# Second attention layer: context read feature-major from DRAM instead of transposed on TensorE

## Chip, cores and metric

The kernel runs on one core of one Trainium2 chip, as one launch. The metric is the device time of a run in microseconds, and the time of a version is the median of its runs. All data are float32 except the attention mask bias.

## The reference

A stream `x` of 8 batches x 512 tokens x 512 features goes through four stages, each adding its result to `x`. Two stages are cross-attention to the same context, `ctx_1024`, of 8 batches x 120 keys x 512 features:

```python
x = x + tanh(g_xattn[0]) * L0_xattn(layernorm(x), ctx, ctx)          # 16 heads of 32
x = x + tanh(g_ffn[0])   * L0_ffn(layernorm(x))                      # routed experts
x = x + tanh(g_xattn[1]) * L1_xattn(layernorm(x), ctx, ctx, mask)    # the same, with mask and biases
x = x + tanh(g_ffn[1])   * L1_ffn(layernorm(x))                      # channel mix

# both attention layers, from the same ctx, with their own weights:
k = split_heads(ctx @ Wk.T + bk);  v = split_heads(ctx @ Wv.T + bv)
attn = softmax(q @ k.T / sqrt(32), masked);  out = (attn @ v) @ Wo.T + bo
```

The context does not change between the two layers; only the weights do.

## The kernel before

The four stages run one after the other on the core; `x` (32 tiles of 128 tokens x 512 features) stays in SBUF. `CrossAttention` is built twice, once for each attention layer. Its constructor does what comes before the loop over token tiles: `load` (L260) puts all loads of the layer on the queue of the SP engine, in the order written; `project_keys` (L321) makes the transposed context `ctxT` and from it the transposed keys `kT`; then come the layer-norm of the first tiles, `make_mask`, the sums of query weights on GpSimd (`sum_query_weights`, L426), and `prologue` (L376), which projects the values of a batch at a time (`project_values`, L357) between transposes of `x` and the first queries.

The context arrives token-major: 120 keys on the partitions, 8 batches x 512 features in each (`ctx`, loaded in two halves of four batches, L278). TensorE contracts over partitions, so both projections need the features on the partitions. For each batch, four transposes by the identity (L327) fill one PSUM tile `ctps`, and a copy takes it to `ctxT`: on VectorE for even batches (L334), on ScalarE for odd ones (L332). After every fourth batch, the keys of these four batches are computed (L342): four PSUM tiles `kps`, each of four matmuls of 480 columns, evicted by ScalarE (L351 in the second layer, L355 in the first). `project_values` later uses the same `ctxT` as the stationary operand, a batch at a time (L361).

In the constructor of either layer the order of all engines is the written one (`tc.manual_schedule(engines=every)`): each engine takes its instructions in this order, and an instruction that waits holds back what is behind it. SBUF pools are stacked: `ctx`, `wk` and `mrow` lie in a pool (`at_k`) that is given up after `project_keys` and the mask, `ctxT` and `bv` in one (`at_v`) given up after the prologue. A load into a place that was in use before waits for its last user. In the second layer these users are those of the expert stage that ends just before: its matmuls `l2ps` (L959), the transposes `rps` (L992), the scatter matmuls `ops` with `permT` (L1013) and the updates of `x` after them (L1021).

Other names that matter: `wv`, `wq`, `wo`, `wk` are the layer's weights, 1 MB each; `bqk`, `bv`, `gbo` its biases; `mrow` the mask, from which VectorE makes `mbias` (L316). `stats_of_batch` runs the layer-norm sums of four tiles on VectorE (L49, L50) and their scales on GpSimd (L58 to L64). `normalize` makes `xn` on ScalarE (L406), and in the second layer GpSimd then adds the output bias to `x` (L410). `queries` multiplies by `wq` and its sums (L149).

Of the kernel before, what the change touches and what calls it, by code (L numbers as in the profile page):

```python
# [9 lines left out]
FP = mybir.dt.float32  # L10
I32 = mybir.dt.int32
BF = mybir.dt.bfloat16
AF = mybir.ActivationFunctionType
# [4 lines left out]
P = 128  # L18
B, S, D = 8, 512, 512
LK = 120  # L20
# [3 lines left out]
NC = D // P  # L24
# [3 lines left out]
SM_SCALE = 1.0 / math.sqrt(HD)  # L28
# [178 lines left out]
class CrossAttention:  # L207
# [5 lines left out]


    def __init__(
        self, cm, tc, es, ins, gate, mask=None, biases=None, loads=(), then=None, vpool=None
    ):
        self.cm, self.nc, self.tc, self.gate, self.then = cm, cm.nc, tc, gate, then
        self.masked, self.biased = mask is not None, biases is not None
        nc = cm.nc  # L220

        def pool(name, bufs, **kw):
            pool = tc.tile_pool(name=name, bufs=bufs, reuse_waits="tile", **kw)
            return es.enter_context(pool)

        self.pool = pool("at_w", 1)
        vpool = vpool or self.pool
        self.norm = pool("at_n", 2)
        self.soft = pool("at_soft", 2)
        self.p_mm = pool("at_mm", 4, space=PSUM)  # L230
        self.p_s = pool("at_s", 2, space=PSUM)
        self.wq = self.pool.tile([P, NC, D], FP, name="wq")
        self.wo = self.pool.tile([P, NC, D], FP, name="wo")
        self.kT = self.pool.tile([P, NC, B * LK], FP, name="kT")
        self.v = [vpool.tile([P, 2, D], FP, name=f"v{q}") for q in range(B // 2)]
        self.xn, self.xnT, self.qT, self.probs, self.aT = {}, {}, {}, {}, {}
        self.ops = {}

        def right(name):
            return tc.tile_pool(name=name, bufs=1, side="right", reuse_waits="tile")  # L240

        with right("at_v") as self.vp:
            with right("at_k") as self.kp:
                self.load(ins, list(loads), mask, biases)
                if self.biased:
                    self.scale_biases()
                self.project_keys()
                if self.biased:
                    nc.gpsimd.tensor_scalar(self.gbo, self.gbo, self.gate, None, ALU.mult)
                for t in range(2):  # L250
                    self.normalize(t)
                if self.masked:
                    self.make_mask()
                self.sum_query_weights()
                for b in (1, 2):
                    self.stats_of_batch(b)
            self.work = pool("at_work", 2)
            self.prologue()

    def load(self, ins, loads, mask, biases):  # L260

        nc, kp, vp = self.nc, self.kp, self.vp
        ctx_in, wqT, wkT, wvT, woT = ins
        self.ctxT = vp.tile([P, NC, B * LK], FP, name="ctxT")

        wv = self.soft.tile([P, NC * D], FP, name="wv", tag="pr")
        self.wv = wv.rearrange("p (c f) -> p c f", c=NC)
        if self.biased:
            self.bv = vp.tile([LK, D], FP, name="bv")
        self.ctx = kp.tile([LK, B, D], FP, name="ctx")  # L270
        self.wk = kp.tile([P, NC, D], FP, name="wk")
        if self.masked:
            self.mrow = kp.tile([P, B, LK], I32, name="mrow")
        ctx_in = ctx_in.rearrange("b k d -> k b d")

        def half(h):
            bs = slice(h * B // 2, (h + 1) * B // 2)
            nc.sync.dma_start(out=self.ctx[:, bs, :], in_=ctx_in[:, bs, :])  # L278

        def weights(w, w_in):  # L280
            nc.sync.dma_start(out=w, in_=w_in.rearrange("(c p) f -> p c f", p=P))

        half(0)
        weights(self.wk, wkT)
        half(1)
        if self.biased:
            bqk_in, bv_in, bo_in = biases
            self.bqk = self.pool.tile([P, 2, NC], FP, name="bqk")
            nc.sync.dma_start(out=self.bqk, in_=bqk_in)
        weights(self.wv, wvT)  # L290
        if loads:
            loads.pop(0)()
        if self.biased:
            nc.sync.dma_start(out=self.bv, in_=bv_in.partition_broadcast(LK))
        if self.masked:
            nc.sync.dma_start(out=self.mrow, in_=mask.partition_broadcast(P))
        if self.biased:
            self.gbo = self.pool.tile([P, D], FP, name="gbo")
            nc.sync.dma_start(out=self.gbo, in_=bo_in.partition_broadcast(P))
        weights(self.wq, wqT)  # L300
        if loads:
            loads.pop(0)()
        weights(self.wo, woT)
        for more in loads:
            more()
# [13 lines left out]


    def project_keys(self):  # L321
        nc, ident = self.nc, self.cm.ident
        half = B * LK // 2
        for b in range(B):
            ps = self.p_mm.tile([P, NC, LK], FP, name="ctps", tag="mm")
            for c in range(NC):
                nc.tensor.transpose(  # L327
                    ps[:, c, :], self.ctx[:, b, c * P : (c + 1) * P], ident[:LK, :LK]
                )
            dst = self.ctxT[:, :, b * LK : (b + 1) * LK]  # L330
            if b % 2:
                nc.scalar.copy(dst, ps)  # L332
            else:
                nc.vector.tensor_copy(dst, ps)  # L334
            if b == B - 1:
                self.stats_of_batch(0)
            if b % 4 == 3:
                h = b // 4
                for f in range(NC):
                    ps = self.p_mm.tile([P, half], FP, name="kps", tag="mm")  # L340
                    for c in range(NC):
                        nc.tensor.matmul(  # L342
                            ps,
                            self.wk[:, c, f * P : (f + 1) * P],
                            self.ctxT[:, c, h * half : (h + 1) * half],
                            start=(c == 0),
                            stop=(c == NC - 1),
                        )
                    dst = self.kT[:, f, h * half : (h + 1) * half]
                    if self.biased:  # L350
                        nc.scalar.activation(  # L351
                            dst, ps, AF.Identity, bias=self.bqk[:, 1, f : f + 1], scale=SM_SCALE
                        )
                    else:
                        nc.scalar.activation(dst, ps, AF.Copy, scale=SM_SCALE)  # L355

    def project_values(self, b):  # L357
        nc = self.nc
# [992 lines left out]
def flamingo_kernel(ctx: ExitStack, tc: tile.TileContext, a: dict, out: bass.AP):  # L1351
    nc = tc.nc
    const = ctx.enter_context(tc.tile_pool(name="const", bufs=1))
    ident = const.tile([P, P], FP, name="ident")
    make_identity(nc, ident)
    gates = const.tile([P, 4], FP, name="gates")
# [9 lines left out]
        )  # L1366

    cm = Common(nc, const, x, ident)

    engines = mybir.EngineType  # L1370
    compute = {engines.PE, engines.DVE, engines.Activation, engines.Pool}
    every = compute | {engines.SP}
    with ExitStack() as es:
        ffn = RoutedFfn(
            cm, tc, es, gates[:, 2:3],
            [a[n] for n in ("wc", "bc", "tie", "w1", "b1", "w2", "b2")],
        )
        loads = [lambda b=b: load_x(b) for b in range(B)]
        with ExitStack() as at:
            with tc.manual_schedule(engines=every):  # L1380
                attention = CrossAttention(
                    cm, tc, at, [a[n] for n in ("ctx", "wq0", "wk0", "wv0", "wo0")],
                    gates[:, 0:1], loads=loads, then=ffn.in_slot,
                    vpool=ffn.vpool,
                )
            with tc.manual_schedule(engines={engines.PE}):
                attention.run()
            with tc.manual_schedule(engines=compute):
                attention.tail()
        ffn.run()  # L1390
    with ExitStack() as es:
        mix = ChannelMix(
            cm, tc, es, [a[n] for n in ("wr", "wk", "wv", "mu")], gates[:, 3:4], out
        )
        with tc.manual_schedule(engines=every):
            attention = CrossAttention(
                cm, tc, es, [a[n] for n in ("ctx", "wq1", "wk1", "wv1", "wo1")],
                gates[:, 1:2], a["mask"], (a["bqk"], a["bv"], a["bo"]), then=mix.in_slot,
            )
        with tc.manual_schedule(engines={engines.PE, engines.SP}):  # L1400
            attention.run()
        with tc.manual_schedule(engines=compute):
            attention.tail()
            mix.run()
# [63 lines left out]
```

## Time and profile before

| | us |
|---|---|
| median of 3 runs | 1436.9 (1434.19 to 1437.84) |
| the profiled execution, own time | 1433.48 |
| its span, first to last instruction | 1431.7 |
| start of the second layer's key stage (its first transposes) | 690.65 |
| end of that stage (first value matmul) | 721.58 |

The span is cut into what each engine did. Busy times, of the span: TensorE matmuls 97%, VectorE 72%, ScalarE 54%, GpSimd 45%. The mean granted TensorE clock is 0.998. The 16 DMA engines moved 69.46 MB, most of it at the start and between the stages. The second layer's loads land in two bursts: `ctx` and `wk` from 664.68 on, when the last `l2ps` matmul lets them, and `wv` to `wo` between 688.60 and about 705.

A line of a timeline or of a chain begins with the start and the length of a piece in us; "x16" counts instructions. A float32 matmul leaves two records, so the 16 key matmuls of a half appear as 32. A "chain of waits" is followed back from the last instruction, at each step to what released it.

### The profile page before, as it was taken

The numbers are of one execution on the slowest core, as the hardware profiler recorded it, in microseconds if no ns is written. First come the engines' busy times: TensorE is split into PE (matmuls) and PEld (weight loads), VectorE is DVE, ScalarE is ACT, GpSimd is POOL, SyncE is SP. The second block draws the span as 40 slices with busy tenths as digits, with TensorE's granted clock in tenths as the row PEclk, the third lists the DMA queues.
The fourth block names the chain that finished last, engine by engine and source line by source line (L and its number), as shares of the span: only waits on it lengthen the run. The fifth ranks groups of instructions, "written<-read, shape, count | busy, mean of one in ns | idle before, by whom it ended". The sixth has DMA issues, their size and how long they took to land.

```text
span 1431.7 us, 32559 instructions
## 1 busy us (share of the span) xinstructions
PE 1384.2 (97%) x13728; PEld 1068.2 (75%) x13728; DVE 1025.1 (72%) x1457; ACT 772.3 (54%) x1874; POOL 643.9 (45%) x576
## 2 busy tenths in 40 slices
PE   7999999999999998999999999999998999999997
PEld 3577777777776787888557777777776788888886
DVE  2666777777777676777576777777778588887786
ACT  1256666666666445444225665666656555445543
POOL 1425545545443001555375665665646333343331
PEclk9999999999999999999999999999999999999999
DMA  9200000000001347433301000000000000000001
GB/s 300 107 9 24 24 23 23 24 23 16 24 31 46 127 135 231 120 105 87 117 0 60 2 1 2 1 2 2 2 30 2 1 30 30 31 30 30 30 16 45
DMA packets 44886, 69.46 MB, mean 49 GB/s; under 512 B 2891, under 2 KB 20811, under 8 KB 44739
## 3 DMA queue, kind: packets, MB, share of 16 engines
q1 hardware_dynamic: 44451, 67.37, 14.6%
q8 instruction: 108, 1.77, 0.5%
q14 instruction: 39, 0.32, 0.1%
q10 hardware_dynamic: 288, 0.00, 0.0%
HBM read 50.59 MB, written 16.78 MB: 47 GB/s over the span
## 4 chain that ended last, share of the span: by engine, by line
PE 72%; DVE 14%; ACT 6%; POOL 4%; issue 3%; DMA 1%; POOLq 0%; DVEq 0%; ACTq 0%
PE ops L598 15%; PE qps L149 13%; PE tps L546 6%; PE cps L149 5%; PE aps L581 5%; PE s L489 4%; PE kps L342 4%; PE rps L992 3%; PE vps L361 3%; PE rlps L731 2%; PE l1ps L907 2%; PE ops L1013 2%; PE xnps L421 2%; PE l2ps L959 2%; PE gps L880 2%
## 5 line engine op out<-in xcount | busy, mean ns | idle before, releaser
L507 POOL TENSOR_TENSOR pr<-pr,rs 128x960 f32<-128x960 f32 x128 | 228.8, 1790 | 251.9 <-DVE rs L506 233.5
L598 PE MATMUL ops<-wo,aT 128*128 128x512 f32 x512 | 239.6, 594 | 0.7 <-ACT aT L589 0.7
L517 ACT ACTIVATE pr<-s,nmx 128x120 f32<-128x120 f32 x512 | 177.4, 372 | 114.0 <-DVE nmx L514 107.8
L598 PEld LDWEIGHTS ops<-wo,aT 128*128 128x128 f32 x512 | 92.1, 190 | 71.9 <-issue 67.0
L1005 POOL TENSOR_TENSOR r<-r,b 128x1024 f32<-128x1024 f32 x31 | 73.5, 2377 | 142.6 <-ACT r L1004 142.6
L149 PE MATMUL qps<-xnT,wq 128*128 128x256 f32 x512 | 119.6, 381 | 0.0
L546 PEld LDWEIGHTS tps<-ident,pr 128*120 128x120 f32 x864 | 96.8, 138 | 29.5 <-issue 26.2
L525 DVE TENSOR_REDUCE mx<-s 128x8 f32<-128x960 f32 x64 | 74.0, 1156 | 56.9 <-PE s L489 56.9
L517 ACT ACTIVATION_READ_ACCUMULATOR pr<-s,nmx 128x1 f32 x512 | 111.3, 217 | 0.0
L546 PE MATMUL tps<-ident,pr 128*120 128x128 f32 x864 | 104.7, 273 | 2.5 <-ACT pr L517 1.4
L149 PEld LDWEIGHTS qps<-xnT,wq 128*128 128x128 f32 x512 | 95.7, 189 | 15.2 <-issue 1.0
L533 DVE TENSOR_REDUCE sm<-pr 128x8 f32<-128x960 f32 x64 | 73.6, 1150 | 22.1 <-ACT pr L528 22.0
L49 DVE BATCH_NORM_STATS2 bnst<-x 128x6 f32<-128x512 f32 x128 | 86.8, 678 | 1.3
L422 ACT COPY xnT<-xnps 128x512 f32<-128x512 f32 x64 | 38.1, 595 | 82.0 <-PE xnps L421 82.0
L514 DVE TENSOR_REDUCE nmx<-s 128x8 f32<-128x960 f32 x64 | 73.5, 1149 | 6.8 <-PE s L489 6.8
L581 PE MATMUL aps<-prT,v 120*32 120x128 f32 x2048 | 73.3, 278 | 4.5 <-ACT prT L571 2.6
L527 DVE TENSOR_TENSOR pr<-s,mx 128x960 f32<-128x960 f32 x64 | 73.6, 1150 | 0.9
L1258 POOL TENSOR_TENSOR x<-x,cv 128x512 f32<-128x512 f32 x28 | 41.4, 1479 | 70.8 <-DVE cv L1255 70.8
L556 ACT COPY prT<-tps 120x1024 f32<-120x1024 f32 x54 | 55.0, 1019 | 32.9 <-PE tps L546 32.9
L489 PE MATMUL s<-kT,qT 32*128 32x120 f32 x2048 | 71.4, 276 | 0.0
L489 PEld LDWEIGHTS s<-kT,qT 32*128 32x128 f32 x2048 | 66.1, 187 | 6.5 <-issue 6.3
L581 PEld LDWEIGHTS aps<-prT,v 120*32 120x32 f32 x2048 | 53.8, 110 | 18.8 <-issue 8.3
(189 smaller groups left out, 3101.1 us busy)
## 6 DMA issues: line engine op xcount, KB each, us to landing
w<-in_w_dram SPq DMA_DIRECT2D x32, 512.0 KB, 4.8
x<-in_x_dram SPq DMA_DIRECT2D x8, 1024.0 KB, 15.4
aside<-x SPq DMA_DIRECT2D x32, 256.0 KB, 2.0
x<-aside SPq DMA_DIRECT2D x8, 1024.0 KB, 9.8
out_dram<-x SPq DMA_DIRECT2D x14, 512.0 KB, 2.8
ctx<-in_ctx_dram SPq DMA_DIRECT2D x4, 960.0 KB, 11.8
wk<-in_wk_dram SPq DMA_DIRECT2D x3, 1024.0 KB, 11.1
wv<-in_wv_dram SPq DMA_DIRECT2D x3, 1024.0 KB, 5.5
```

Of the source, the lines that this page charges most:

```text
L49: cm.nc.vector.bn_stats(st, cm.x[:, t, :])
L149: self.nc.tensor.matmul(ps[:, m, :], self.a[a][:, k, m * P : (m + 1) * P], self.b[b][:, k, :], start=(k == 0), stop=(k == 1),)
L489: nc.tensor.matmul(s[j // 2][:, j % 2, hc * LK : (hc + 1) * LK], self.qT[b][r : r + 32, hc, toks], self.kT[r : r + 32, hc, keys], start=no ...
L507: nc.gpsimd.tensor_tensor(pr[:, js, :, :], pr[:, js, :, :], rs[:, js, :, :].to_broadcast([P, 2, NC, LK]), ALU.mult,)
L514: nc.vector.tensor_reduce(nmx, sv[1], AX.X, ALU.max, negate=True)
L517: nc.scalar.activation(pr[:, 2 + j, hc, :], sv[1][:, j, hc, :], AF.Exp, bias=nmx[:, j, hc, :], accum_out=sm[:, 2 + j, hc : hc + 1],)
L525: nc.vector.tensor_reduce(mx, sv[0], AX.X, ALU.max)
L527: nc.vector.tensor_tensor(pv, sv[0], mx.to_broadcast([P, 2, NC, LK]), ALU.subtract)
L533: nc.vector.tensor_reduce(sm[:, :2, :], pv, AX.X, ALU.add)
L546: nc.tensor.transpose(ps[:, jj, hc * P : (hc + 1) * P], pr[:, 2 * u + jj, hc, :], self.cm.ident,)
L581: nc.tensor.matmul(aps[32 * j : 32 * j + 32, hc, :], self.v[b // 2][:LK, b % 2, h * HD : (h + 1) * HD], prT[:, j, hc, :], start=True, stop ...
L598: nc.tensor.matmul(ops, self.aT[t][:, c, :], self.wo[:, c, :], start=(c == 0), stop=(c == NC - 1),)
```

## The change

The first layer writes its `ctxT` (128 partitions x 3840 elements, 1.97 MB) to a DRAM tile `aside`, as the last thing of its `project_keys`. The second layer (`turned`, true where no `loads` are given) does not read the input context. Its two halves of `ctx` are now feature-major, [128, 4, 960], read from `aside` (960 KB each, 480 elements per row and chunk), and serve the key projection in place of `ctxT`. The whole of `aside` is read once more, into `ctxT`, for the value projection; this load stands behind `wv` and ahead of `bv`, `mrow`, `gbo`, `wq` and `wo` on SP. The transposes move into a function `turn_context` that only the first layer calls. The matmuls, their order and the evictions to `kT` are as before.

```diff
+        self.aside, self.turned = aside, not loads
...
+        if self.turned:
+            self.ctx = kp.tile([P, NC, B * LK], FP, name="ctx")
+        else:
+            self.ctx = kp.tile([LK, B, D], FP, name="ctx")
...
         def half(h):
+            if self.turned:
+                keys = slice(h * B * LK // 2, (h + 1) * B * LK // 2)
+                nc.sync.dma_start(out=self.ctx[:, :, keys], in_=self.aside[:, :, keys])
+                return
             bs = slice(h * B // 2, (h + 1) * B // 2)
             nc.sync.dma_start(out=self.ctx[:, bs, :], in_=ctx_in[:, bs, :])
...
         weights(self.wv, wvT)
+        if self.turned:
+            nc.sync.dma_start(out=self.ctxT, in_=self.aside)
         if loads:
             loads.pop(0)()
...
     def project_keys(self):
...
-        for b in range(B):
...
-            if b == B - 1:
+        for h in range(2):
+            if not self.turned:
+                for b in range(h * B // 2, (h + 1) * B // 2):
+                    self.turn_context(b)
+            if h == 1:
                 self.stats_of_batch(0)
-            if b % 4 == 3:
-                h = b // 4
-                for f in range(NC):
...
+            ctxT = self.ctx if self.turned else self.ctxT
+            for f in range(NC):
...
+        if not self.turned:
+            self.nc.sync.dma_start(out=self.aside, in_=self.ctxT)
+
+    def turn_context(self, b):
+        nc = self.nc
+        ps = self.p_mm.tile([P, NC, LK], FP, name="ctps", tag="mm")
+        for c in range(NC):
+            nc.tensor.transpose(
+                ps[:, c, :], self.ctx[:, b, c * P : (c + 1) * P], self.cm.ident[:LK, :LK]
+            )
+        dst = self.ctxT[:, :, b * LK : (b + 1) * LK]
+        if b % 2:
+            nc.scalar.copy(dst, ps)
+        else:
+            nc.vector.tensor_copy(dst, ps)
...
+    dram = ctx.enter_context(
+        tc.tile_pool(name="ctx_turned", bufs=1, space=bass.MemoryType.DRAM)
+    )
+    aside = dram.tile([P, NC, B * LK], FP, name="turned")
```

Both constructor calls pass `aside` on. The key matmuls of a half and their evictions are moved unchanged into the new loop.

More of the change, by code (lines that the diff above doesn't have):

```diff
@@ L215, in __init__ @@
     def __init__(
-        self, cm, tc, es, ins, gate, mask=None, biases=None, loads=(), then=None, vpool=None
+        self, cm, tc, es, ins, gate, aside, mask=None, biases=None, loads=(), then=None,
+        vpool=None,
     ):
@@ L269, in load @@
             self.bv = vp.tile([LK, D], FP, name="bv")
-        self.ctx = kp.tile([LK, B, D], FP, name="ctx")
+        if self.turned:
+            self.ctx = kp.tile([P, NC, B * LK], FP, name="ctx")
+        else:
+            self.ctx = kp.tile([LK, B, D], FP, name="ctx")
         self.wk = kp.tile([P, NC, D], FP, name="wk")
@@ L321, in project_keys @@
     def project_keys(self):
-        nc, ident = self.nc, self.cm.ident
         half = B * LK // 2
-        for b in range(B):
[L325 to L334, printed above, removed]
-            if b == B - 1:
-                self.stats_of_batch(0)
-            if b % 4 == 3:
-                h = b // 4
-                for f in range(NC):
[L340 to L355, printed above, removed]
@@ new lines, in project_keys @@
+        for h in range(2):
[3 more added lines that the diff above has]
+            if h == 1:
+                self.stats_of_batch(0)
+            ctxT = self.ctx if self.turned else self.ctxT
+            for f in range(NC):
+                ps = self.p_mm.tile([P, half], FP, name="kps", tag="mm")
+                for c in range(NC):
+                    self.nc.tensor.matmul(
+                        ps,
+                        self.wk[:, c, f * P : (f + 1) * P],
+                        ctxT[:, c, h * half : (h + 1) * half],
+                        start=(c == 0),
+                        stop=(c == NC - 1),
+                    )
+                dst = self.kT[:, f, h * half : (h + 1) * half]
+                if self.biased:
+                    self.nc.scalar.activation(
+                        dst, ps, AF.Identity, bias=self.bqk[:, 1, f : f + 1], scale=SM_SCALE
+                    )
+                else:
+                    self.nc.scalar.activation(dst, ps, AF.Copy, scale=SM_SCALE)
@@ new lines, in project_keys @@
+        if not self.turned:
[3 more added lines that the diff above has]
+        ps = self.p_mm.tile([P, NC, LK], FP, name="ctps", tag="mm")
+        for c in range(NC):
+            nc.tensor.transpose(
+                ps[:, c, :], self.ctx[:, b, c * P : (c + 1) * P], self.cm.ident[:LK, :LK]
+            )
+        dst = self.ctxT[:, :, b * LK : (b + 1) * LK]
+        if b % 2:
+            nc.scalar.copy(dst, ps)
+        else:
+            nc.vector.tensor_copy(dst, ps)
@@ L1368, in flamingo_kernel @@
     cm = Common(nc, const, x, ident)
+    dram = ctx.enter_context(
+        tc.tile_pool(name="ctx_turned", bufs=1, space=bass.MemoryType.DRAM)
+    )
+    aside = dram.tile([P, NC, B * LK], FP, name="turned")
     engines = mybir.EngineType
@@ L1382, in flamingo_kernel @@
                     cm, tc, at, [a[n] for n in ("ctx", "wq0", "wk0", "wv0", "wo0")],
-                    gates[:, 0:1], loads=loads, then=ffn.in_slot,
+                    gates[:, 0:1], aside, loads=loads, then=ffn.in_slot,
                     vpool=ffn.vpool,
@@ L1397, in flamingo_kernel @@
                 cm, tc, es, [a[n] for n in ("ctx", "wq1", "wk1", "wv1", "wo1")],
-                gates[:, 1:2], a["mask"], (a["bqk"], a["bv"], a["bo"]), then=mix.in_slot,
+                gates[:, 1:2], aside, a["mask"], (a["bqk"], a["bv"], a["bo"]), then=mix.in_slot,
             )
```

## The prediction

> **What bounds the kernel now.** I read the page's list of busy times first, then the chain of waits, cut to the stretch in which the second layer begins.
>
> ```profile
> span 1431.7 us, 32559 instructions
> ...
> PE 1384.2 (97%) x13728; PEld 1068.2 (75%) x13728; DVE 1025.1 (72%) x1457; ACT 772.3 (54%) x1874; POOL 643.9 (45%) x576
> ...
> PE 72%; DVE 14%; ACT 6%; POOL 4%; issue 3%; DMA 1%; POOLq 0%; DVEq 0%; ACTq 0%
> ```
>
> TensorE (PE) works 97% of the span and is 72% of the chain, DMA 1%. So time is to be had where PE does or awaits something that can go. The chain in the window 686 to 726 us (start, length, what):
>
> ```profile
> 688.73 1.94 PE ops L1013 x60
> 690.67 1.86 PE ctps L327 x16
> 692.52 0.02 issue
> 692.55 0.57 ACT ctxT L332
> 693.12 0.04 issue
> 693.16 13.15 PE kps L342 x32
> 706.31 1.66 PE ctps L327 x16
> 707.96 0.02 issue
> 707.99 0.57 ACT ctxT L332
> 708.55 0.04 issue
> 708.60 13.15 PE kps L342 x32
> 721.75 3.45 PE vps L361 x8
> ```
>
> From the last scatter matmul to the first value matmul the chain is nothing but PE, and twice the copy for which PE stands still. Twice the same three steps: sixteen transposes, the last copy to `ctxT`, the keys. None of this waits for a transfer. PE's timeline gives the starts without the pipelined ends:
>
> ```profile
> 690.65 1.86 PE L327 MATMUL ctps<-ident,ctx 120*128 120x120 f32 x16
> 693.16 1.07 PE L342 MATMUL kps<-ctxT,wk 128*128 128x480 f32 x2 [0.65 <-ACT ctxT L332]
> ...
> 706.14 1.80 PE L327 MATMUL ctps<-ident,ctx 120*128 120x120 f32 x16
> 708.60 1.07 PE L342 MATMUL kps<-ctxT,wk 128*128 128x480 f32 x2 [0.65 <-ACT ctxT L332]
> ```
>
> **What is removed.** In the second layer: 32 transposes with their weight loads, four VectorE copies (656 ns mean) and four ScalarE copies (561 ns). From the first transpose to the first key matmul: 693.16 - 690.65 = 2.51 us; in the second half 708.60 - 706.14 = 2.46. Both lie whole on PE's path. The copies count only in the 0.65 us waits inside these figures; elsewhere VectorE and ScalarE stand idle for PE here. Sum of the removal: **-4.97 us**. The keys themselves stay: 12.98 us a half from start to start (693.16 to 706.14, 708.60 to 721.58), so I put them at 690.65 to 703.63 and 703.63 to 716.61, and the first value matmul at 716.61.
>
> May the keys start at 690.65? They need the first half of `ctx` and `wk`. Issued at 664.68 and 665.08, these landed after 7.2 and 12.2 us, by 677.3; the second half (665.59, 15.1 us) by 680.7, and it is needed at 703.6. The pieces become 1920 bytes on 128 partitions instead of 2048 on 120, the bytes are the same, and the loads wait for the same last `l2ps`. Slack 13 us and 23 us: cost nothing. The PSUM banks: the first transposes already waited 0.2 us for an update of `x` (L1021) in VectorE; the first keys take the same bank behind the same wait: nothing.
>
> **What is added.** (a) The first layer writes 1.97 MB to DRAM. It is issued after the last load of `x` (SP is done issuing at 36.3 us), the engines move 387 GB/s from 36 to 40 us and are idle after about 46; the write is some 5 us at that rate. Next on SP is `wc`, which waited 51.2 us for PE and issued at 87.62. If the write mixed with the last loads of `x`, these would land up to 5 us later, near 51; the last batch's sums run at 61. Hidden; nothing.
>
> (b) The second layer loads 1.97 MB more, into `ctxT`, and five loads stand behind it on SP:
>
> ```profile
> 688.60 0.61 SPq L281 DMA_DIRECT2D wv<-in_wv_dram  x1
> 689.43 0.36 SPq L294 DMA_DIRECT2D bv<-in_bv_dram  x1
> 690.71 0.34 SPq L296 DMA_DIRECT2D mrow<-in_mask_dram  x1
> 691.10 0.42 SPq L299 DMA_DIRECT2D gbo<-in_bo_dram  x1
> 691.58 0.42 SPq L281 DMA_DIRECT2D wq<-in_wq_dram  x1
> ```
>
> `ctxT` takes over the place of `permT`, so it waits for the last scatter matmul, to 690.7. `mrow` waited for that already, so SP loses only the issue, some 0.4 us. The transfer: 295 GB/s (mean of 690 to 704 us) make 6.7 us, which I take, as it is the rate of the very burst that the load joins; 387 GB/s make 5.1; the slowest 1 MB row of the page that shares no long queue, `x<-aside` (1024 KB in 9.8 us), makes 18.4. So everything behind lands 5.1 to 18.4 us later:
> - `ctxT` itself: behind `wv` (688.60 + 5.5 = 694.1) by 701, at worst near 712.5; needed at 716.6.
> - `wq`: landed at 691.58 + 10.7 = 702.3, now 709 (720.7); GpSimd's weight sums began at 725.88, now 720.9.
> - `mrow`: 696.2, now 702.9 (714.6). VectorE's `mbias` waits for it, and this and the eight layer-norm sums behind it, 7.0 us together, must be done when the first value eviction is due, at 725.22 - 4.97 = 720.25. At 6.7 us it fits (710); at 18.4 it is 1.4 us late.
> - `gbo`: 698.5, now 705.2 (716.9), needed with its 1.57 us scaling at 718.3: at worst 0.2 late.
> - `bv`: at worst 715, needed at 720.25; `wo` is needed only at 786.
>
> Cost 0 as I take it, 1.4 at the worst bound.
>
> **What is moved.** VectorE's sums of batch 0 no longer stand behind the copies and run at about 691 instead of 708; one of them now goes ahead of the last update of `x` (0.75 us), for which no key matmul waits. ScalarE's `xn` and GpSimd's bias additions follow the last key eviction, so they move up with PE.
>
> **Does the gain live on?** PE is then busy without a break to 748. There it waits 1.1 us, named after GpSimd's scales, while VectorE's query sums run slow beside GpSimd (1.72 us instead of 0.69). That group hangs on the transposed `x`, on `xn` and on the value evictions, which all follow PE; so it moves as a block and the wait stays. If it vanished, 1.1 more would be won. Sum: -4.97, bounds -3.6 and -6.1. The span becomes 1426.7, the profiled time 1433.48 - 4.97 = 1428.5; the median of the runs lies 3.4 above that profiled time, so I predict **1431.9** (1436.9 - 5.0), with bounds 1430.8 to 1433.3 and, by the spread of the runs shown (2.7 below the median, 0.9 above), 1428.1 to 1434.2.
>
> **Rivals.**
> - *The next wait takes it.* If GpSimd's work from 723.28 on (back to back to 750) or VectorE's sums were tied to a landing or to each other and did not move, PE would wait longest at 749 and all 5.0 go: 1436.9; half moved, 1434.4. For it: GpSimd is busy 8.59 of the 10 us from 735 to 745, VectorE 9.65. Against: both begin with something that PE's evictions release (`xn` at 722.34, `v` at 725.22), and VectorE idled 6.9 us before that.
> - *The loads are late: slower.* The added transfer holds up `wq` in SP's queue, GpSimd's in-order weight sums start late, and with them all scales behind, up to the queries. It begins to cost at 720.9 - 702.3 = 18.6 us of added landing time and makes the kernel slower than before at 23.6 us, 83 GB/s. At half the rate of the slowest row (36.8 us) it would be 36.8 - 18.6 - 5.0 = 13.2 us slower: 1450. No row is below 107 GB/s, so little speaks for it. By the Trainium skill (TensorE: Matmul & The Clock Gate, Part 1), a PE that idles for a window of about 3.4 us runs at half rate until it has been busy about as long, which by our estimate would add up to 1.7 us here. The trace agrees in part: after 9.3 us of idleness at the start the first sixteen transposes took 3.29 us against 1.80 later, though the granted clock's row reads 1.00 there.
> - *It doesn't do what it says.* The second layer is built without `loads`, so it skips the transposes by its own condition. If they stayed, the added loads alone would leave 1436.9.
>
> **Chances.** Forecast 0.81, next wait 0.13, late loads 0.05, nothing done 0.01. Changes within 0.3% (4.3 us) can't be told from none here. The forecast's 5.0 is only just beyond: with medians that move by one or two us I give it four in five to be seen as faster. Faster 0.81 x 0.79 = 0.64; slower 0.05, the late loads; within 0.3% the rest, 0.31. Range: from 1428.1 up over half of the next-wait case, to 1435.5.
>
> **What would show it.** Keys of the second layer starting within 0.3 us of the end of the scatter and running 26.0 us without a gap; value matmuls 26 us after the scatter, not 30.9; no wait for `ctxT`, `wq` or `mrow`; the wait at the first queries still about 1 us; the first layer unchanged; the span shorter by 4.5 to 5.5 us. A PE wait for a DMA in the second layer, or one above 2 us at the first queries, would prove the forecast wrong.

## The result, and the profile after

Ten runs of the changed kernel have a median of 1430.28 us (1426.89 to 1434.47), ten of the kernel before beside them 1437.22 (1434.19 to 1440.13). The ratio is 0.9955, 95% interval 0.994 to 0.997: 6.5 us faster, between 4.3 and 8.6. Eight further runs against twenty of the kernel before gave 1429.85 against 1435.76, ratio 0.9954 (0.9938 to 0.997). The forecast was 1431.9, 5.0 less than before.

The profiled execution of the changed kernel took 1431.72 us. Its page first: the span, the busy time and count of each engine, the shares of the chain.

```profile
span 1429.9 us, 32488 instructions
...
PE 1383.4 (97%) x13696; PEld 1067.2 (75%) x13696; DVE 1020.5 (71%) x1453; ACT 768.2 (54%) x1870; POOL 644.0 (45%) x576
...
PE 72%; DVE 14%; ACT 6%; POOL 4%; issue 3%; DMA 1%; POOLq 0%; SPq 0%; DVEq 0%; ACTq 0%
```

The page shows what is gone: 32 transposes on PE and their 32 weight loads (PEld), four copies on VectorE, four on ScalarE. The totals say nothing of where time was won; that is in the chain of waits at the start of the second layer (start, length, what).

```profile
691.33 1.94 PE ops L1031 x60
693.27 26.01 PE kps L345 x64
719.28 3.45 PE vps L379 x8
```

The six pieces of before, with two waits for a copy between them, have become one. From the end of the scatter to the first value matmul it was 721.75 - 690.67 = 31.08 us and is 719.28 - 693.27 = 26.01: **5.07 us less**. PE's timeline of the same stretch has no idle time in front of the keys:

```profile
691.33 1.94 PE L1031 MATMUL ops<-r,permT 128*32 128x128 f32 x60 [0.30 <-POOL r L1023]
693.25 26.03 PE L345 MATMUL kps<-ctx,wk 128*128 128x480 f32 x64
```

The scatter ends 2.6 us later here than in the profile of before. PE's timeline finds these 2.6 us in the expert stage, between 537 and 549 us, before any edited line of the second layer runs (last section).

The list of waits from 680 to 800 us (engine, line, what it waited for; us, times, longest) has two waits for a load that the profile of before did not have:

```profile
DVE mbias L328 <- DMA mrow<-in_mask_dram: 8.3, 1, 8.3
...
POOL gbo L252 <- DMA gbo<-in_bo_dram: 7.6, 1, 7.6
...
PE qps L149 <- POOL nmr L64: 1.1, 1, 1.1
```

VectorE and GpSimd now wait for the two loads behind the added one, 8.3 and 7.6 us, but PE does not. From the first value matmul to the first query products with sums there are 27.5 us in both profiles, and the 1.1 us wait there is the same.

### The profile page after: what moved, and what is told of

Same layout as the page of the kernel before. It is cut to its first block, busy times and chain, and to the rows that moved or that the text cites. A ratio compares the mean times of both kernels' runs of the same rounds, so it can differ in the third digit from the quotient of the medians.

```text
span 1429.9 us, 32488 instructions
## 1 busy us (share of the span) xinstructions
PE 1383.4 (97%) x13696; PEld 1067.2 (75%) x13696; DVE 1020.5 (71%) x1453; ACT 768.2 (54%) x1870; POOL 644.0 (45%) x576
## 3 DMA queue, kind: packets, MB, share of 16 engines
q8 instruction: 108, 1.77, 0.5%
## 4 chain that ended last, share of the span: by engine, by line
PE 72%; DVE 14%; ACT 6%; POOL 4%; issue 3%; DMA 1%; POOLq 0%; SPq 0%; DVEq 0%; ACTq 0%
PE ops L616 15%; PE qps L149 13%; PE tps L564 6%; PE cps L149 5%; PE aps L599 5%; PE s L507 4%; PE kps L345 4%; PE rps L1010 3%; PE vps L379 3%; PE l1ps L925 2%; PE rlps L749 2%; PE ops L1031 2%; PE gps L898 2%; PE xnps L439 2%; DVE rT L990 2%
## 6 DMA issues: line engine op xcount, KB each, us to landing
x<-in_x_dram SPq DMA_DIRECT2D x8, 1024.0 KB, 15.4
```

## The experiments

All kernels but those that say otherwise are edits of the changed kernel. "Key stage" is the figure above, read from the chain of each kernel's profile: 31.08 before, 26.01 after. All times are medians.

**The traffic without the gain**, and **half of the gain**. The first keeps the token-major context and the transposes in the second layer, writes the context aside in the first, and reads the 1.97 MB back behind `wv`, not into `ctxT` but into the places of `wq` and `wo`, which are overwritten later:

```diff
-            nc.sync.dma_start(out=self.ctxT, in_=self.aside)
+            spare = self.aside.rearrange("p c k -> p (c k)")
+            for w, at, n in ((self.wq, 0, 2048), (self.wo, 2048, 1792)):
+                w = w.rearrange("p c f -> p (c f)")
+                nc.sync.dma_start(out=w[:, :n], in_=spare[:, at : at + n])
...
-            if not self.turned:
-                for b in range(h * B // 2, (h + 1) * B // 2):
-                    self.turn_context(b)
+            for b in range(h * B // 2, (h + 1) * B // 2):
+                self.turn_context(b)
```

> The second layer loads the token-major context and transposes it as before, but the first layer writes its transposed context to DRAM and the second reads the 1.97 MB back behind wv (into the places of wq and wo, whose own loads then follow), so all added transfers are there and nothing is removed. Theory (the gain is the two blocks of transposes and copy waits on TensorE's path; the transfers are hidden): no change against the kernel before, within 0.3%; first value matmul 30.9 us after the end of the scatter matmuls. Rival (some of the gain came from elsewhere than the transposes, such as faster loads): up to 1.5 us faster than before. Rival (the added transfers cost time that the removal paid for): slower by 1 us or more, with TensorE waits in the first layer or in the second layer's value stage.

1435.22 against 1436.63 (twelve runs, 23 before), ratio 0.9987 (0.9975 to 0.9999). The key stage was 31.07 us, as before. The traffic alone makes nothing slower. The interval even lies just below 1, by 0.1 to 3.6 us, which is what the first rival foretold; this is taken up under "The measure itself".

The second loads only the first half of the keys feature-major and transposes the second:

```diff
-            if not self.turned:
+            if not self.turned or h == 1:
                 for b in range(h * B // 2, (h + 1) * B // 2):
...
-            ctxT = self.ctx if self.turned else self.ctxT
+            first = self.turned and h == 0
+            ctxT = self.half0 if first else self.ctxT
```

> Only the first half of the second layer's context (batches 0 to 3) comes feature-major from DRAM; the second half is loaded token-major and transposed. Theory: half of the gain, 2.51 us, so the first value matmul comes 28.4 us after the scatter (30.9 before, 26.0 with the whole change), and the time lies 2.5 us under the kernel before. Rival (the gain hangs on the way in which the stage begins, not on the transposes): the whole gain or none.

1431.76 (twelve runs), ratio 0.9967 (0.9955 to 0.9978). The chain of its profile:

```profile
691.78 1.94 PE ops L1038 x60
693.73 13.13 PE kps L350 x32
706.85 1.66 PE ctps L371 x16
708.51 0.02 issue
708.53 0.57 ACT ctxT L378
709.10 0.04 issue
709.14 13.15 PE kps L350 x32
722.29 3.45 PE vps L386 x8
```

722.29 - 693.73 = 28.56, 2.52 less than before. Each half is worth its own 2.5 us.

**The added load at the end of the queue.** `ctxT` is issued behind `wo` in place of ahead of `bv`:

```diff
         weights(self.wv, wvT)
-        if self.turned:
-            nc.sync.dma_start(out=self.ctxT, in_=self.aside)
...
         weights(self.wo, woT)
+        if self.turned:
+            nc.sync.dma_start(out=self.ctxT, in_=self.aside)
```

> As the changed kernel, but the second read of the context (into ctxT) is the last load of the layer, behind wo. It should land about 16 us after the end of the scatter, ten before the values need it, and mrow, gbo and wq should land about 4 us earlier than in the changed kernel. Theory (all of them have slack): the same time as the changed kernel, key stage 26.0 us. Rival (the waits of VectorE for mrow and of GpSimd for gbo, 8.3 and 7.6 us in the changed kernel, cost something): faster by up to 1.5 us, with the wait at the first queries under 0.5 us.

1428.24 (four runs), ratio 0.9939 (0.9916 to 0.9962). `ctxT` landed 18.1 us after the scatter, ahead of the values at 26. VectorE's and GpSimd's waits for `mrow` and `gbo` fell to 3.8 and 2.6 us, and PE gained nothing by that: key stage 26.01, then 27.5 to the queries with sums, as in the changed kernel. The two waits were slack; the time itself can't be told from the changed kernel's.

**A load that is really late.** `wq` is loaded nine times in a row on SP, so that it lands 56 us after its first issue:

```diff
-        weights(self.wq, wqT)
+        for _ in range(9 if self.turned else 1):
+            weights(self.wq, wqT)
```

> As the changed kernel, but the second layer loads wq nine times into the same place, each load waiting for the one before, so that its last landing comes some 57 us after the end of the scatter instead of 16. GpSimd's weight sums, due 30.3 us after it, then start 27 us late. The prediction's price (everything behind them on GpSimd is late by as much, and TensorE with it): 27 us slower than the changed kernel. Rival (the scales and bias sums behind them have slack of their own; the second batch's normalisation runs 7 us after its scales, its transposes 6 us after that): 13 to 15 us slower.

1455.93 (four runs), ratio 1.014 (1.012 to 1.016): 25.7 us above the changed kernel. The waits of its profile from 690 to 800 us, and then the same stretch in windows (us; busy time of each engine, granted PE clock, DMA share, GB/s):

```profile
POOL wqs L88 <- DMA wq<-in_wq_dram: 27.7, 1, 27.7
...
PE qps L149 <- DMA wq<-in_wq_dram: 9.6, 1, 9.6
...
PE s L508 <- DVE qT L198: 6.0, 1, 6.0
```

```profile
744.00:756.00 12.00, 4.00 (x10) 3.22 (x11) 0.00 (x0) 0.00 (x0) 3.83 (x4) 0.58 0.65 234
756.00:763.00 7.00, 2.38 (x12) 1.61 (x10) 2.24 (x4) 3.66 (x7) 6.17 (x11) 0.99 0.00 0
763.00:767.00 4.00, 3.46 (x10) 2.88 (x11) 1.15 (x3) 0.25 (x1) 3.34 (x9) 0.58 0.01 4
767.00:780.00 13.00, 8.87 (x64) 7.54 (x62) 1.50 (x3) 4.38 (x7) 12.17 (x18) 1.00 0.00 1
780.00:787.00 7.00, 5.10 (x21) 2.69 (x22) 5.36 (x6) 0.18 (x1) 5.16 (x4) 0.51 0.00 0
```

GpSimd's weight sums were due at 724.2 and began 27.7 us later; the kernel lost 25.7. Beyond its slack this load cost nearly one for one, as the rival of late loads had it. PE waits only 9.6 us for the load itself; the rest follows. The queries with sums come 16.1 us later after the first value matmul than in the changed kernel, and 10.1 more go by the first product of probabilities and values (`aps`): GpSimd works off what stood behind its sums (12.17 busy of 13 us from 767 to 780), and three of the stretches after PE's idleness show a granted clock of 0.58, 0.58 and 0.51. Of the 10.1 us, 8.2 lie ahead of the eight value matmuls (16 records) at 783.06, where the chain of waits runs through GpSimd alone from 751.94 to 781.14, so they are the backlog; the other 1.9 are these matmuls themselves, which fall into the stretch at 0.51 and take 8.83 us from start to start in place of 6.96. The rule named in the prediction (the Trainium skill, TensorE: Matmul & The Clock Gate, Part 1) agrees here: PE stands idle from 742.4 to 752.0 us, the half clock shows from 745.9 on, and the clock is back at 756.1, 4 us after PE works again.

**Only the order of the transposes.** The kernel before, with all 32 transposes of the second layer ahead of its keys:

```diff
-            if b % 4 == 3:
-                h = b // 4
+            halves = (b // 4,) if b % 4 == 3 else ()
+            if self.masked:
+                halves = (0, 1) if b == B - 1 else ()
+            for h in halves:
```

> The kernel before, but all 32 transposes of the second layer are made ahead of all its keys, so that only one of the two waits for a last copy is left. Theory (each half costs 1.8 us of transposes and 0.65 us of waiting): from the scatter to the first value matmul 30.5 us in place of 31.2, one wait of 0.65 us for the copy in place of two. Rival (the copies hide behind the next transposes only while the PSUM banks last): with eight sets of transposes in a row TensorE waits for a free bank, and the stage takes 31.2 us or more.

```profile
692.58 3.48 PE ctps L327 x32
696.07 25.77 PE kps L344 x64
721.84 3.45 PE vps L363 x8
```

721.84 - 692.58 = 29.26, 1.82 less than before, where I had counted 0.65. Two waits of 0.65 us make 1.3 of it; the other 0.5 lie in the breaks between transposes and keys, for by PE's timeline the keys take 25.77 us in one piece in place of twice 12.98, and the rest is at the transposes. The first half's copies are hidden behind the second half's transposes, and the first keys need only these, so no wait is left at all; the second half's copies hide behind the first keys. PE did not run out of PSUM banks. Timed, too:

> The kernel before with all 32 transposes of the second layer ahead of its keys, now timed. Theory (the profile of it showed the key stage 1.83 us shorter, since both waits for a copy vanish): 1434.5, ratio 0.9987. Rival (the shorter stage is given back later, in the values or the queries): 1436.3, ratio 1.000.

1432.48 against 1435.76 (twelve runs, twenty before), ratio 0.9978 (0.9965 to 0.9991): 3.2 us faster, between 1.3 and 5.0. So 1.82 of the 5.07 us were to be had without a byte of traffic. Only 5.07 - 1.82 = 3.25 needs the transposes to go: their 3.48 in this chain, less 0.24 by which the keys' piece of the chain is longer where it stands directly behind the scatter (26.01 against 25.77).

**The wait at the first queries.** Beside the 1.1 us the prediction named VectorE's sums of the queries, which run slow beside GpSimd. Three kernels try to take that slowness away. The first makes the layer-norm sums of all eight batches in the key stage, where VectorE stood idle:

```diff
-                self.stats_of_batch(0)
+                for b in range(B if self.turned else 1):
+                    self.stats_of_batch(b)
...
-                for b in (1, 2):
+                for b in () if self.turned else (1, 2):
...
-        if b + 3 < B:
+        if b + 3 < B and not self.turned:
```

> Theory (the 1.1 us for which TensorE waits at the first queries is VectorE's doing: its sums of the queries run slowly beside GpSimd while it still has layer-norm sums of later batches to make): with the sums of all eight batches moved into the key stage, where VectorE stands idle, the wait falls below 0.3 us, from the first value matmul to the first queries 26.4 to 26.8 us in place of 27.5, and the time is 1.1 us below that of the changed kernel, near 1429. Rival (the wait is GpSimd's own, by its scales): the wait stays at 1.1 us and so does the time, near 1430.3. A third way: the earlier sums delay the value evictions, TensorE waits inside the values, and the time is longer.

1429.1 (eight runs), ratio 0.9961 (0.9946 to 0.9976). That the median is the theory's 1429 is chance: the ratio is no lower than the changed kernel's, 0.9955. The wait was still 1.1 us, and from the first value matmul to the queries 27.5; only its name had changed, from GpSimd's scales to VectorE's sums. Next, GpSimd's addition to the sixth tile was written later, directly ahead of that to the seventh:

```diff
-        if self.biased:
-            nc.gpsimd.tensor_tensor(cm.x[:, t, :], cm.x[:, t, :], self.gbo, ALU.add)
+        due = {TB + 1: (), TB + 2: (TB + 1, TB + 2)}.get(t, (t,))
+        for i in due if self.biased else ():
+            nc.gpsimd.tensor_tensor(cm.x[:, i, :], cm.x[:, i, :], self.gbo, ALU.add)
```

> As with the early layer-norm sums, and GpSimd's bias addition to the sixth tile of x, which ran beside VectorE's second query sum, is held back until that of the seventh. Theory (that sum takes 1.77 us in place of 0.69 because GpSimd adds beside it, and this is the 1.1 us wait of TensorE): the sum takes 0.69, the wait at the first query products with sums falls below 0.1 us, from the first value matmul to the first queries with sums 1.1 us less, and the time is 1.1 us below that of the early sums alone, near 1428. Rival (the sum is slow for another reason, or something else comes due at the same moment): the wait stays at 1.1 us and the time near 1429.1 to 1430.3.

1429.25 (seven runs), ratio 0.9957 (0.9938 to 0.9975), wait 1.1 us. But the trace shows an addition to `x` at 742.18 as before, released by ScalarE's `xn`, and the sum beside it still at 1.78 us: the addition did not move. No other instruction of GpSimd stands between its old place and the new one, and it waits only for the sixth `xn`, so the edit left GpSimd's order as it was, and this run tells nothing of the wait. The last kernel leaves that one addition out (the output is without the output bias of the second layer for the sixth tile of 128 tokens):

```diff
-        if self.biased:
+        if self.biased and t != TB + 1:
```

> As with the early layer-norm sums, and the bias addition to the sixth tile of x in the second layer (GpSimd, one instruction of 1.27 us) is left out, so that GpSimd is idle while VectorE makes the second query sum. Theory (that sum takes 1.77 us in place of 0.69 because GpSimd adds beside it, and this is TensorE's wait of 1.1 us): the sum takes 0.7 us, the wait at the first query products with sums falls below 0.1 us, from the first value matmul to these 26.4 us in place of 27.5, and the time is 1.1 us below that of the early sums alone. Rival (the sum is slow by its own shape, or something else is due at the same moment): the wait stays at 1.1 us, from the first value matmul to the queries 27.5.

1428.59 (six runs), ratio 0.9952 (0.9933 to 0.9971). VectorE's timeline with the early sums alone, then without the addition, and PE's in the latter (in brackets the idle time in front and what ended it):

```profile
740.53 0.69 DVE L107 TENSOR_TENSOR xns<-xnT 128x512 f32<-128x512 f32 x1 [0.36 <-ACT xnT L441]
741.33 1.77 DVE L107 TENSOR_TENSOR xnT<-xnT 128x512 f32<-128x512 f32 x1
743.42 0.69 DVE L170 TENSOR_TENSOR qT<-qT,qps 128x512 f32<-128x512 f32 x1 [0.32 <-PE qps L149]
```

```profile
741.24 0.69 DVE L107 TENSOR_TENSOR xnT<-xnT 128x512 f32<-128x512 f32 x1
743.34 0.69 DVE L170 TENSOR_TENSOR qT<-qT,qps 128x512 f32<-128x512 f32 x1 [1.40 <-PE qps L149]
743.95 1.41 DVE L107 TENSOR_TENSOR xnT<-xnT 128x512 f32<-128x512 f32 x2
```

```profile
743.09 0.60 PE L440 MATMUL xnps<-ident,xn 128*128 128x128 f32 x4
744.78 1.97 PE L149 MATMUL qps<-xnT,wqs 128*128 128x256 f32 x8 [1.09 <-DVE xnT L107]
```

Half of the theory holds: without GpSimd beside it the sum takes 0.69 us in place of 1.77. The other half falls: VectorE then stands idle for 1.40 us, and PE waits 1.09 all the same. In VectorE's order the eviction `qT` (L170) stands ahead of the third sum, and it waits for PE's product; then come its 0.69 us and the sum's, and meanwhile PE has only four transposes to do. A third sum ahead of that eviction should take the wait away; this was not tried. The profile of before had shown as much in the first layer, which has no bias additions: both sums take 0.69 us there, and PE waits all the same (VectorE, then PE):

```profile
64.86 0.69 DVE L107 TENSOR_TENSOR xns<-xnT 128x512 f32<-128x512 f32 x1
65.58 0.69 DVE L107 TENSOR_TENSOR xnT<-xnT 128x512 f32<-128x512 f32 x1
67.77 0.69 DVE L170 TENSOR_TENSOR qT<-qT,qps 128x512 f32<-128x512 f32 x1 [1.49 <-PE qps L149]
```

```profile
69.21 1.97 PE L149 MATMUL qps<-xnT,wqs 128*128 128x256 f32 x8 [1.12 <-DVE xnT L107]
```

**The measure itself.** Three kernels ask why most of the kernels gained one to two us more than their key stage. The kernel before, unchanged; the kernel before with the first layer's write alone (the traffic kernel without its reads); and the changed kernel again.

> The kernel before, unchanged, measured as the others are. Theory (the 1.4 to 3.7 us that the changed kernels gained beyond their key stage come of the changed kernels themselves): ratio 1.000, its interval around 1, time near 1436.6. Rival (they come of how the runs are interleaved, the kernel before running in a place where the granted clock is lower): ratio 0.998 to 0.999, 1434 to 1435.

> The first layer writes its turned context to DRAM and nobody reads it; the second layer is that of the kernel before, 31.2 us from the scatter to the first value matmul. Theory (the write and the transfers cost nothing, and what was gained beyond the key stage is not the write's): 1436.6, ratio 1.000 within 0.001. Rival (the write, or the transfer that it adds to the order of the queues, brings the gain beyond the key stage): near 1434.7, ratio 0.9985 to 0.999, as with the traffic alone. If the write cost something, the time would be above 1437.5.

> The changed kernel, unchanged, beside the same runs of the kernel before as the others. Theory (the change is worth its key stage, 5.07 us, and what was measured beyond it is scatter): ratio 0.9965, near 1431.3. Rival (it is worth 6.5 us or more, some of it from a higher granted clock elsewhere): ratio 0.9955 or less, near 1429.9.

| kernel | key stage against before, us | time against before, us (95%) |
|---|---|---|
| before again | 0 | +0.4 (-1.0 to +2.0) |
| write only | 0 | -1.3 (-2.6 to +0.1) |
| traffic only | 0 | -1.9 (-3.6 to -0.1) |
| transposes first | -1.8 | -3.2 (-5.0 to -1.3) |
| first half | -2.5 | -4.7 (-6.5 to -3.2) |
| changed | -5.1 | -6.5 (-8.6 to -4.3) |
| changed again | -5.1 | -6.6 (-8.9 to -4.3) |
| added load last (four runs) | -5.1 | -8.8 (-12.1 to -5.5) |
| early sums | -5.1 | -5.6 (-7.8 to -3.4) |
| early sums, addition written later | -5.1 | -6.2 (-8.9 to -3.6) |
| early sums, addition left out | -5.1 | -6.9 (-9.6 to -4.2) |

(The times are the ratio less one, times the median of before in the same comparison.) The times follow the key stage, but every edited kernel lies 0.5 to 3.7 us beyond it, with or without the write, and the unchanged one does not. Each interval holds the key stage's figure or misses it by at most 0.7 us. So the write alone isn't shown to be the cause (the kernel with the transposes first has no added traffic and lies 1.4 us beyond), nor is a bias of the comparison. By its ratio of 0.9954 the changed kernel, run again, came out at its rival's figure and not at the theory's 0.9965, which its interval still holds; the write alone, at 0.9991, lies between its theory's 1.000 and its rival's 0.9985 to 0.999, and its interval holds both. The kernel before has a mean granted clock of 0.9968 over the runs that have one on record (79), the changed one 0.9974 (18), and among the runs of the kernel before one with 0.001 more is 1.1 us shorter. By that some 0.7 of the changed kernel's 1.4 us go with the clock, as an estimate. That does not explain them, for an idle PE lowers the clock too, as the late load showed. What brings the excess stays open; the profiles' segments outside the key stage scatter by more than this from run to run.

## Why the prediction was right, step by step

- *The bound.* Right. The key stage was PE's alone, and what left it left the time: 5.07 us in the profile, 2.52 for one half.
- *The removal.* Predicted -2.51 and -2.46, a sum of -4.97; the chain shows -5.07, and PE's timeline, from which the prediction was read, 30.93 - 25.87 = 5.06. The 0.1 us beyond the sum are the keys, which I put at twice 12.98 us and which take 25.87 in one piece, directly behind the scatter and without a gap.
- *"The copies count only in the 0.65 us waits inside these figures."* Right, and the run with the transposes first shows how much hung on the order rather than on the work: 1.82 us, of which the two waits are 1.3.
- *(a), the write.* Hidden, as predicted. It was issued at 36.33 us behind the last load of `x`; `wc` behind it was issued at 87.58 (87.62 before); the first layer's first queries with sums begin at 69.21 us in both profiles; with the write alone the time was not above that of before.
- *(b), the second read: the size was off.* "295 GB/s make 6.7 us, which I take": the delay is not one number. Counted from the end of the scatter, `mrow` landed 6.4 us later than before and `gbo` 5.3, but `wq` only 4.2 (15.8 us in place of 11.6), below my lower bound of 5.1. So for the load that the late-loads rival hangs on the term was too large; I had moved the whole burst by one transfer time, but the engines moved 331 and 252 GB/s in the first 8 us of that burst before, and 347 and 374 after. They had room that the added load filled. Nothing hung on it, since the delay stayed within the slack; the load at the end of the queue, which takes most of the delay away, gains PE nothing.
- *"No wait for `ctxT`, `wq` or `mrow`": wrong in part.* VectorE waited 8.3 us for `mrow`, and GpSimd 7.6 for `gbo`. The batch sums ahead of them had moved up, as I had written, so the engines came to these loads sooner while the loads came later; I set the landing against the time when it is needed and did not say that the engines would stand and wait. On PE there was none.
- *The wait at the first queries* stayed at 1.1 us and moved with PE, as predicted. VectorE's slow sum, which I named beside it, does not set it.
- *Rivals.* The next wait took nothing: 27.5 us from the values to the queries in all kernels but that with the late `wq`. The late-loads rival was wrong in its condition and right in its price beyond that: 27.7 us late at GpSimd, 25.7 us longer. Against it I wrote that "No row is below 107 GB/s". That is wrong: on the page of before `ctx` (960 KB in 11.8 us) makes 83 GB/s, the very rate at which the rival turns the kernel slower, and the first loads of `x` (1024 KB in 15.4 us) make 68. The added load itself made 197 (1920 KB in 10.0 us). And the granted clock of 1.00 that I read for the first transposes is no measurement: the trace's first record of the clock begins at 12.3 us, 3.0 us after the first transpose.
- *The total.* 5.0 predicted, 6.5 measured, the interval 4.3 to 8.6 holding both 5.0 and 5.07. The 1.4 us between are not in the key stage.
- *"The span shorter by 4.5 to 5.5 us": wrong for the two profiles.* Theirs differ by 1.8 (1431.7 and 1429.9). Of the 5.07, 2.6 were lost ahead of the key stage and 1.1 near 1087 us, where PE runs at half clock for 6.8 us in place of 3.4 (last section); 0.4 came back in small pieces. From the key stage up to there the gain held: the second layer's products start 2.5 us earlier at the first queries with sums (746.64 against 749.08) and 2.6 earlier at 1077 us. The medians, not this pair, carry the forecast.

## What to carry to other kernels

A piece of work that stands alone on the chain of the busiest engine is worth its full length, but look at its parts: more than a third of this one (1.82 of 5.07 us) were two waits for a copy and the breaks around them, which another order removes without moving a byte. Price an added transfer by the room that the queue has when it comes and by when the loads behind it are due, not by the transfer's own time; here it cost nothing inside the slack, and beyond it nearly one for one. A wait named after one engine's slow instruction is proved only by making that instruction fast: here it became 1.1 us shorter and the wait remained.

## What the hardware showed beside that

The profiled execution of the changed kernel lost the 2.6 us of its later scatter in a stage without an edit. PE's timeline and the windows there:

```profile
540.17 1.85 PE L898 MATMUL gps<-perm,x 32*128 32x128 f32 x57 [2.58 <-issue]
542.44 1.17 PE L898 MATMUL gps<-perm,x 32*128 32x128 f32 x32 [0.42 <-DVE pT L913]
544.97 4.28 PE L925 MATMUL l1ps<-pT,w 128*32 128x128 f32 x88 [1.36 <-ACT pT L915]
```

```profile
536.00:540.00 4.00, 1.46 (x39) 1.09 (x36) 2.21 (x2) 1.96 (x2) 0.00 (x0) 1.00 1.19 300
540.00:544.00 4.00, 3.02 (x89) 2.64 (x88) 2.71 (x3) 2.17 (x3) 0.00 (x0) 1.00 0.70 215
544.00:548.00 4.00, 3.03 (x65) 3.06 (x69) 0.87 (x1) 0.77 (x1) 0.00 (x0) 0.67 0.02 5
```

The kernel before has the same three idle times there, but the first is shorter:

```profile
538.99 1.84 PE L880 MATMUL gps<-perm,x 32*128 32x128 f32 x56 [1.40 <-issue]
```

Beside a DMA share of 1.19 PE stood for 2.58 us with nothing that the profile shows to wait for, and after three short idle times (2.58, 0.42 and 1.36 us within 7.4 us) the granted clock fell to 0.67 in the window, though none of them alone is as long as the 3.4 us that the Trainium skill gives as the clock gate's window (TensorE: Matmul & The Clock Gate, Part 1). The records put the half clock there at 3.4 us; in the profile of before the clock stayed at 1.00. So 1.2 of the 2.6 us are the longer idle time, and the other 1.4 fall where the clock is halved. The first idle time ends 1.3 us (before: 1.4) after a 16 KB packet of the queue that the page calls "instruction" has landed, at 538.9 us here and at 537.6 before; that PE waited for its own instructions is likely by that, but not shown.

A like stretch near 1087 us lasts 3.4 us in the profile of before, 6.8 in that of the changed kernel, and is missing in those of the bias addition written later or left out. The thirteen profiles other than that of the late load have 0 to 10.2 us of half clock between the start and the end. With the gain of each one's key stage added back, their spans are 1430.4 to 1431.6 us where there is none (three), 1431.2 to 1434.6 with 3.4 us (five), 1433.7 with 6.8 (one) and 1435.0 to 1437.7 with 10.2 (four). So much of what single executions differ by goes with these stretches, and that is the reason why a gain of 5 us is read from a stage and not from two spans. What brings the stretches in some executions and not in others of the same kernel was not found.
